# Second-layer row terms by way of VectorE and DRAM in place of TensorE, from batch 18 on

## The chip, the cores and the metric

The kernel runs on one core of a Trainium2 chip. The core has a matrix engine (TensorE, PE in the profile, with its weight loads as PEld), a vector engine (VectorE, DVE), an activation engine (ScalarE, ACT), a general-purpose engine (GpSimd, POOL) and SyncE (SP), which here issues most DMAs. Each engine runs its own instructions in order and waits on semaphores. DMAs from all queues share 16 DMA engines. The metric is the device time of one execution in microseconds; the comparison is between medians of several runs.

## The reference

The input `x` is 64 batches of 256 rows by 256 columns, with one 256x256 adjacency matrix for all. Two layers follow each other; in each, a graph attention and then a feed-forward part are added to `x`, each fed by a layer norm. What matters here is the attention of the second layer:

```
h = matmul(inp, W)                                  # 256 x 256 per batch
e_src = h @ a1;  e_dst = h @ a2                     # one number per row
e = leaky_relu(e_src[:, :, None] + e_dst[:, None, :], 0.01)
e = where(adj == 0, -1e9, e)
h_prime = matmul(softmax(e, -1), h);  out = relu(h_prime)
```

The feed-forward part of the first layer is a linear map, that of the second a mixture of eight experts of which each row uses its best two. All numbers are 32-bit floats.

## The kernel before

A batch is held as two row tiles of 128 rows (`NT` = 2) and two column tiles (`KT` = 2). The function `batch_layers` (L594) is a generator that does all of one batch's attention and linear work; its `yield` values are ranks. A main loop (L1241) advances in steps. Every third step a new batch starts, and in each step every active generator advances once, in the order of the ranks: a positive rank ends its part of the step, a negative one puts it back into the same step's queue at that rank. So the order of instructions on each engine is fixed when the program is built, several batches overlap, and the ranks alone set it. Three batches' stages stand in one round of three steps.

The row terms. Since exp is monotone, exp(leaky_relu(s + d)) is the larger of two products, exp(s)exp(d) and exp(0.01 s)exp(0.01 d). With a factor pulled out, each score is `max(term_of_column_row, number_of_partition) * mask`. The first operand of the max must be a row of 256 numbers that is the same in all 128 partitions, though `projected1` (L497) makes it as one number per partition (`ex[:, t, 1]`, L511). `scores1` (L520) turns it round: for each of the two tiles TensorE transposes the column, broadcast along the free axis to 128x128, against the identity into a PSUM bank `pd` (L523). VectorE then makes the scores of both tiles (L528), with `pd`, the partition's own number and the pre-scaled mask `me` (L517).

The first layer, with four heads, does the same thing by another way for all but the first batch. VectorE transposes the terms in 32x32 blocks into a small tile `ut` (L537, `send_terms`), a DMA stores them in DRAM (L621) and a second DMA reads the stored row into all 128 partitions at once with a stride of zero (L554, `rows_to_all`, 512 KB), into the last part of the score tile `z` that it is later overwritten in. Then VectorE makes the scores (L570). From batch 18 on (`SETTLED`, L129) both DMAs go through SP's queue, before that through ScalarE's.

Around the scores. VectorE's order in one round is, in the settled part: the scaling of the first layer's q (L485), the transpose L537, the statistics of a newer batch (L378, L379), the expert outputs y (L993), the expert inputs' transposes sT (L117), the second layer's scores (L528), the first layer's attention results (L591, L639), the second layer's residual (L694), the linear part's result x2 (L667), and so on to the first layer's scores (L570). ScalarE takes the exponential of L639's result (L645), the weighting of y (L961), the squares for the norm of x2 (L424) and the copy of the transposed x2 (L459). TensorE multiplies that copy in L504 (`projected1`), and then continues with the first layer's projection (L469), expert products (L968 hidden, L983 out), the transposes L523 and the attention sums (L584).

SP's order in one round: x in blocks (L106), the store of the terms (L621), the next x (L96), the read of the terms (L554), the store of a base (L734), then the loads of two expert pairs (L906 in four parts, L917, and their weights L935). A DMA of SP also waits for the DMA that stands eight before it.

Of the kernel before, what the change touches and what calls it, by code (L numbers as in the profile page):

```python
# [9 lines left out]
F32 = mybir.dt.float32  # L10
I32 = mybir.dt.int32
AF = mybir.ActivationFunctionType
ALU = mybir.AluOpType
AX = mybir.AxisListType

P = 128
# [5 lines left out]
def rows_to_all(ap: bass.AP, n: int) -> bass.AP:  # L22

    return bass.AP(tensor=ap.tensor, offset=ap.offset, ap=[[0, P], [1, n]])
# [3 lines left out]
def kernel(  # L28
# [17 lines left out]
    nc = tc.nc  # L46
    B, N, D = x.shape
# [4 lines left out]
    NT = N // P  # L52
# [21 lines left out]
    work = ctx.enter_context(tc.tile_pool(name="work", bufs=2))  # L74
    small = ctx.enter_context(tc.tile_pool(name="small", bufs=4))
# [3 lines left out]
    def bank(name, shape):  # L79
        t = psum.tile([P, 2 * D], F32, tag="bank", name=name, bufs=8)  # L80
        n = 1
        for s in shape:
            n *= s
        t = t[:, :n]
        if len(shape) == 2:
            t = t.rearrange("p (a b) -> p a b", a=shape[0])
        elif len(shape) == 3:
            t = t.rearrange("p (a b c) -> p a b c", a=shape[0], b=shape[1])
        return t
# [22 lines left out]
    S = 32  # L112
    G = P // S
# [15 lines left out]
    SETTLED = CHUNKS[0] + CHUNKS[1] + CHUNKS[2] + CHUNKS[3] + 2  # L129


    ident = const.tile([P, P], F32, tag="ident", name="ident")
# [186 lines left out]
    def once(work):  # L319
# [14 lines left out]
        out=tri, in_=tri, pattern=[[1, P]], base=0, channel_multiplier=-1,  # L334
# [157 lines left out]
    for i in range(2):  # L492
        t = keep.tile([P, NT, D + 1], F32, tag=f"q1_{i}", name=f"q1_{i}")
# [3 lines left out]
    def projected1(xT, rstd, b):  # L497

        q = q1s[b % 2]
        pqs = []  # L500
        for t in range(NT):
            pq = bank("pq", [D + 3])
            for k in range(KT):
                nc.tensor.matmul(  # L504
                    pq, xT[:, k, t * P : (t + 1) * P], wx1[:, k, :],
                    start=(k == 0), stop=(k == KT - 1),
                )
            pqs.append(pq)
        ex = small.tile([P, NT, 3], F32, tag="ex1", name="ex1")
        for t, pq in enumerate(pqs):  # L510
            nc.scalar.activation(ex[:, t, :], pq[:, D:], AF.Exp, scale=rstd[:, t : t + 1])  # L511
            nc.scalar.activation(
                q[:, t, :D], pq[:, :D], AF.Copy, scale=rstd[:, t : t + 1]
            )
        me = work.tile([P, NT, N], F32, tag="me", name="me", bufs=1)
        for j in range(NT):
            nc.scalar.activation(me[:, j, :], masks[1][:, j, :], AF.Copy, scale=ex[:, j, 0:1])  # L517
        return q, ex, me

    def scores1(ex, me):  # L520
        pd = bank("pd", [N])
        for t in range(NT):
            nc.tensor.transpose(  # L523
                pd[:, t * P : (t + 1) * P], ex[:, t, 1:2].to_broadcast([P, P]), ident
            )
        z = work.tile([P, NT, N], F32, tag="z1", name="z1", bufs=1)
        for j in range(NT):
            nc.vector.scalar_tensor_tensor(  # L528
                z[:, j, :], pd, ex[:, j, 2:3], me[:, j, :], op0=ALU.max, op1=ALU.mult
            )  # L530
        return [z[:, j, :] for j in range(NT)]

    def send_terms(q, b):


        ut = small.tile([P, S], F32, tag="ut", name="ut", bufs=1)
        nc.vector.transpose(  # L537
            ut.rearrange("p (t h w) -> p t h w", t=NT, h=H), q[:, :, :, HD - 1 : HD + 3]
        )
        ud = tc.dram_tile([S, S], F32, name=f"terms_{b}")  # L540
        ud = ud.rearrange("c r -> (c r)").rearrange("(c p) -> c p", p=P)
        return ut, ud
# [51 lines left out]
    def batch_layers(b, c0, xng, lg):  # L594
# [23 lines left out]
        if b:  # L618
            ut, ud = send_terms(q, b)
            yield -31  # L620
            terms_queue(b).dma_start(  # L621
                out=ud.rearrange("c (g r) -> g c r", g=G),
                in_=ut[2 : P : S // (NT * H), :],
            )
            yield -52
        z = work.tile([P, NT, NT, H, P], F32, tag="z4", name="z4", bufs=2)
# [17 lines left out]
        ex = work.tile([P, NT, D], F32, tag="e", name="e", bufs=1)  # L644
# [21 lines left out]
        for t in range(NT):  # L666
            nc.vector.scalar_tensor_tensor(  # L667
                x2[:, t, :], pf[:, t, :], rstd[:, t : t + 1], x1b[:, t, :],
                op0=ALU.mult, op1=ALU.add, accum_out=sums[:, t : t + 1],
# [6 lines left out]
        xT = transposed(x2)  # L676
        yield 20
        q, ex, me = projected1(xT, rstd, b)
        yield 25
        z = scores1(ex, me)  # L680
        yield 40
        pvs, rinv = attended(
            q[:, :, None, :], 1, lambda j, h, t: z[j][:, t * P : (t + 1) * P]
# [9 lines left out]
        for t in range(NT):  # L693
            nc.vector.scalar_tensor_tensor(  # L694
                x2[:, t, :], x2[:, t, :], 1.0, rel[:, t, :],
                op0=ALU.mult, op1=ALU.add, accum_out=sums[:, t : t + 1],
# [36 lines left out]
        if not dense:  # L733
            d = nc.sync.dma_start(  # L734
                out=out_rows[b * N : (b + 1) * N, :].rearrange("(t p) d -> p t d", p=P), in_=base
# [476 lines left out]
    def jobs():  # L1212
        b = done = taken = 0
        for c, nb in enumerate(CHUNKS + (1,) * DENSE):
            nt = nb * NT
            lg = keep.tile([P, nt, E], F32, tag="lg", name=f"lg_{c}", bufs=7)
            xng = []
            row0 = b * N
            done += nt
            n = max(done - (E - 1) - taken, 0) if b < ROUTED else 0  # L1220
            taken += n
            for i in range(nb):
                def job(b=b, c=c, i=i, nb=nb, nt=nt, n=n, lg=lg, xng=xng, row0=row0):
                    yield from batch_layers(b, i * NT, xng, lg)
                    if i == nb - 1:
                        if b >= ROUTED:
                            yield 65
                            yield from route_dense(b, lg)
                        else:
                            yield from route(c, row0, nt, n, b == ROUTED - 1, xng, lg)  # L1230
                yield job()
                b += 1
# [85 lines left out]
```

## Time and profile before

| | |
|---|---|
| median of 3 runs | 1486.76 us (1486.3 to 1491.11) |
| profiled execution | 1489.83 us |
| its span | 1488.0 us |
| granted TensorE clock | 0.985 of full |
| busy, share of span | PE 95%, PEld 85%, DVE 83%, ACT 68%, POOL 58% |
| L523, transposes `pd` | 128, mean 278 ns |
| L528, scores of the second layer | 128, mean 460 ns |
| L537, block transposes of the first layer | 63, mean 212 ns |
| L570, scores of the first layer, from z | 504, mean 482 ns |

Busy times are of one profiled execution. A record of a matmul is longer than its share of the engine, since matmuls overlap; what one costs in a dense stretch is the distance between starts. Instructions that only issue DMAs or wait are not counted as busy. In lists of waits the name behind the arrow is what came last.

### The profile page before, as it was taken

The numbers are of one execution on the slowest core, as the hardware profiler recorded it, in microseconds if no ns is written. First come the engines' busy times: TensorE is split into PE (matmuls) and PEld (weight loads), VectorE is DVE, ScalarE is ACT, GpSimd is POOL, SyncE is SP. The second block draws the span as 40 slices with busy tenths as digits, with TensorE's granted clock in tenths as the row PEclk, the third lists the DMA queues.
The fourth block names the chain that finished last, engine by engine and source line by source line (L and its number), as shares of the span: only waits on it lengthen the run. The fifth ranks groups of instructions, "written<-read, shape, count | busy, mean of one in ns | idle before, by whom it ended". The sixth has DMA issues, their size and how long they took to land. (4 is left out here: it accounts for less than half of the span.)

```text
span 1488.0 us, 29865 instructions
## 1 busy us (share of the span) xinstructions
PE 1420.1 (95%) x8138; PEld 1264.0 (85%) x8138; DVE 1232.9 (83%) x4320; ACT 1006.5 (68%) x2389; POOL 864.6 (58%) x851
## 2 busy tenths in 40 slices
PE   6899999999999999999999999999999999899994
PEld 5688888898999999899999989888888888778883
DVE  7689999988898889899888989998888888765442
ACT  1377667577777777777777787777777878643330
POOL 2122446455857676666758585776666668544444
PEclk9899999999999999999999999999999999999998
DMA  4832243567878777787877687768877786988743
GB/s 128 227 98 86 89 130 117 146 172 153 199 171 193 161 177 170 171 185 180 190 156 190 147 193 168 190 164 186 193 158 172 153 173 128 213 201 150 152 66 49
DMA packets 354081, 236.10 MB, mean 159 GB/s; under 512 B 246260, under 2 KB 316156, under 8 KB 353916
## 3 DMA queue, kind: packets, MB, share of 16 engines
q1 hardware_dynamic: 301000, 157.90, 42.1%
q0 software_dynamic: 48864, 66.33, 23.9%
q10 hardware_dynamic: 4052, 9.98, 2.3%
q8 instruction: 67, 1.10, 0.3%
q14 instruction: 98, 0.80, 0.2%
HBM read 146.00 MB, written 88.09 MB: 157 GB/s over the span
## 5 line engine op out<-in xcount | busy, mean ns | idle before, releaser
L1004 POOL DMA_INDIRECT out_dram<-y,xt x258 | 415.6, 1611 | 214.6 <-issue 54.6
L584 PE MATMUL pv<-q,z 128*128 128x65 f32 (+1 forms) x2560 | 363.7, 297 | 0.7 <-DVE z L570 0.3
L584 PEld LDWEIGHTS pv<-q,z 128*128 128x128 f32 x2560 | 331.2, 193 | 13.3 <-DVE z L570 1.3
L1066 POOL DMA_INDIRECT xs<-xng,pos x244 | 256.3, 1050 | 65.2 <-issue 57.7
L983 PE MATMUL py<-w2s,hT 128*128 (+1 forms) x1224 | 282.9, 382 | 4.7 <-ACT hT L974 4.5
L983 PEld LDWEIGHTS py<-w2s,hT 128*128 128x128 f32 x1224 | 229.7, 191 | 37.2 <-ACT hT L974 7.4
L570 DVE SCALAR_TENSOR_TENSOR z<-z,q,mask 128x256 f32<-128x256 f32 x504 | 231.5, 482 | 15.5 <-DMA z<-terms 6.5
L968 PE MATMUL ph<-sT,we 128*128 128x256 f32 x1032 | 241.4, 383 | 1.6 <-DVE sT L117 0.9
L968 PEld LDWEIGHTS ph<-sT,we 128*128 128x128 f32 x1032 | 195.6, 192 | 28.7 <-DVE sT L117 1.4
L961 ACT ACTIVATE y<-y,w 128x256 f32<-128x256 f32 x258 | 113.4, 499 | 119.4 <-DVE y L993 119.2
L459 ACT COPY xT<-pt 128x512 f32<-128x512 f32 x209 | 121.2, 588 | 82.1 <-PE pt L453 80.0
L974 ACT ACTIVATE hT<-ph,we 128x256 f32<-128x256 f32 x306 | 124.1, 472 | 64.1 <-PE ph L968 46.7
L406 POOL TENSOR_SCALAR rstd<-mv 128x4 f32<-128x4 f32 (+1 forms) x66 | 15.9, 240 | 224.8 <-DVE mv L379 175.3
L504 PE MATMUL pq<-wx,xT 128*128 128x259 f32 x512 | 126.5, 390 | 13.9 <-ACT xT L459 13.9
L424 ACT ACTIVATE off<-x,sums 128x256 f32<-128x256 f32 x256 | 129.2, 505 | 9.2 <-DVE x L667 3.3
L993 DVE TENSOR_TENSOR y<-py,b2s 128x512 f32<-128x512 f32 x129 | 86.9, 687 | 56.3 <-PE py L983 44.8
L469 PE MATMUL pq<-wx,xT 128*128 128x268 f32 x512 | 128.1, 394 | 2.4 <-DVE xT L117 1.2
L504 PEld LDWEIGHTS pq<-wx,xT 128*128 128x128 f32 x512 | 96.0, 192 | 33.6 <-ACT xT L459 19.8
L660 PE MATMUL pf<-wfT,xT 128*128 128x256 f32 x512 | 124.2, 386 | 0.0
L469 PEld LDWEIGHTS pq<-wx,xT 128*128 128x128 f32 x512 | 97.9, 192 | 21.7 <-DVE xT L117 1.4
L688 ACT ACTIVATE rel<-pv,rinv 128x256 f32<-128x256 f32 x128 | 54.0, 469 | 82.1 <-DVE rinv L591 81.8
L660 PEld LDWEIGHTS pf<-wfT,xT 128*128 128x128 f32 x512 | 94.9, 196 | 10.6
(170 smaller groups left out, 2355.7 us busy)
## 6 DMA issues: line engine op xcount, KB each, us to landing
we<-wpack SPq DMA_DIRECT2D x145, 288.0 KB
xr<-xs SPq DMA_DIRECT2D x516, 64.0 KB
z<-terms SPq DMA_DIRECT2D x46, 512.0 KB
xin<-in_x_dram SPq DMA_DIRECT2D x64, 256.0 KB
out_dram<-base SPq DMA_DIRECT2D x61, 256.0 KB
xblk<-in_x_dram SPq DMA_DIRECT2D x188, 64.0 KB
z<-terms ACTq DMA_DIRECT2D x17, 512.0 KB
out_dram<-y,xt POOLq DMA_INDIRECT x258
```

Source lines behind the costliest of these rows:

```text
L424: nc.scalar.activation(off, src[:, t, :], AF.Square, bias=sums[:, t : t + 1], scale=-float(D), accum_out=sq[:, at + t : at + t + 1],)
L459: nc.scalar.copy(dst, pt)
L469: nc.tensor.matmul(pq.rearrange("p h c -> p (h c)"), xT[:, k, t * P : (t + 1) * P], wx[:, k, :], start=(k == 0), stop=(k == KT - 1),)
L504: nc.tensor.matmul(pq, xT[:, k, t * P : (t + 1) * P], wx1[:, k, :], start=(k == 0), stop=(k == KT - 1),)
L570: nc.vector.scalar_tensor_tensor(z[:, j, :, h, :], terms, q[:, j, h, HD + 2 : HD + 3], masks[0][:, j, :].rearrange("p (t i) -> p t i", t=N ...
L584: nc.tensor.matmul(pv[:, h, :], z(j, h, t), q[:, j, h, : d + 1], start=(j == 0), stop=(j == NT - 1),)
L660: nc.tensor.matmul(pf[:, t, :], xT[:, k, t * P : (t + 1) * P], wfT[:, k, :], start=(k == 0), stop=(k == KT - 1),)
L968: nc.tensor.matmul(ph[:, f, :], we[:, k * D + f * P : k * D + (f + 1) * P], xT[:, k, :], start=(k == 0), stop=(k == KT - 1),)
L974: nc.scalar.activation(hT[:, f, :], ph[:, f, :], AF.Gelu, bias=we[:, C_B1 + f : C_B1 + f + 1])
L983: nc.tensor.matmul(py[:, t, :], hT[:, f, t * P : (t + 1) * P], w2s[:, e, f * D : (f + 1) * D].rearrange("p e c -> p (e c)"), start=(f == 0 ...
L1004: d = nc.gpsimd.indirect_dma_start(out=out_rows, out_offset=bass.IndirectOffsetOnAxis(ap=xt[:, t, 0:1].bitcast(I32), axis=0), in_=y[:, t, ...
L1066: d = nc.gpsimd.indirect_dma_start(out=xs_d[: E * CAP * PAIR, :], out_offset=bass.IndirectOffsetOnAxis(ap=at, axis=0), in_=xe, in_offset=None,
```

## The change

From batch 18 on the second layer's terms take the way of the first layer's. `scores1` gets the score tile `z` from outside and a flag `spread`, and where it is set it reads the terms from the last part of `z` instead of making `pd`. A new function `turned_terms1` transposes them in blocks on VectorE. Two DMAs on SP's queue are added: a store of 1 KB to a DRAM tile of its own for each batch, and a read of that row into all partitions (128 KB). The order in which VectorE, ScalarE, GpSimd and TensorE work on the rest is the same as before; the block transpose stands behind L537, and on SP the new store stands before the first layer's store, the new read before the first layer's read.

```diff
+    def turned_terms1(ex, b):
+        ut = small.tile([P, S], F32, tag="ut1", name="ut1", bufs=1)
+        nc.vector.transpose(
+            ut.rearrange("p (t w) -> p t w", t=NT),
+            ex[:, :, 1:2].to_broadcast([P, NT, S // NT]),
+        )
+        return ut, tc.dram_tile([N], F32, name=f"terms1_{b}")
...
-    def scores1(ex, me):
-        pd = bank("pd", [N])
-        for t in range(NT):
-            nc.tensor.transpose(
-                pd[:, t * P : (t + 1) * P], ex[:, t, 1:2].to_broadcast([P, P]), ident
-            )
-        z = work.tile([P, NT, N], F32, tag="z1", name="z1", bufs=1)
+    def scores1(ex, me, z, spread):
+        terms = z[:, NT - 1, :]
+        if not spread:
+            terms = bank("pd", [N])
+            for t in range(NT):
+                nc.tensor.transpose(
+                    terms[:, t * P : (t + 1) * P], ex[:, t, 1:2].to_broadcast([P, P]), ident
+                )
         for j in range(NT):
             nc.vector.scalar_tensor_tensor(
-                z[:, j, :], pd, ex[:, j, 2:3], me[:, j, :], op0=ALU.max, op1=ALU.mult
+                z[:, j, :], terms, ex[:, j, 2:3], me[:, j, :], op0=ALU.max, op1=ALU.mult
             )
...
         q, ex, me = projected1(xT, rstd, b)
-        yield 25
-        z = scores1(ex, me)
+        spread = b >= SETTLED
+        if spread:
+            yield -26
+            ut, ud = turned_terms1(ex, b)
+            yield -31
+            nc.sync.dma_start(
+                out=ud.rearrange("(t g r) -> g t r", t=NT, g=G),
+                in_=ut[0 : P : S // NT, :],
+            )
+            yield -52
+        z = work.tile([P, NT, N], F32, tag="z1", name="z1", bufs=1)
+        if spread:
+            nc.sync.dma_start(out=z[:, NT - 1, :], in_=rows_to_all(ud, N))
+        yield 45 if spread else 25
+        z = scores1(ex, me, z, spread)
```

## The prediction

> **What bounds the kernel now.** I read first the busy times by stretch (columns: stretch, busy us and instructions of PE, PEld, DVE, ACT, POOL, granted clock, DMA share, GB/s), then the timeline of one batch in each stretch.
>
> ```profile
> 330.00:931.00 601.00, 601.00 (x3575) 544.52 (x3574) 538.16 (x1840) 460.76 (x1087) 403.93 (x386) 1.00 0.77 175
> 931.00:1214.00 283.00, 274.23 (x1576) 243.13 (x1575) 249.73 (x901) 216.86 (x485) 195.12 (x181) 1.00 0.77 174
> 1214.00:1488.00 274.00, 240.22 (x1152) 207.34 (x1150) 159.14 (x578) 125.15 (x293) 143.05 (x109) 0.96 0.70 139
> ```
>
> Stretch A (batches 18 to 47) has no idle TensorE at all; TensorE is the bound and VectorE has 10% to spare. Stretch B (48 on) has idle TensorE. The rest is a tail, TensorE dense from 1320 to 1440 us, then scatters: time gained or lost in A and B passes through it whole.
>
> What one pair of removed transposes occupies is seen in the timeline of A (start, busy us, instruction):
>
> ```profile
> 707.52 3.62 PE L983 MATMUL py<-w2s,hT 128*128 x16
> 710.98 0.38 PE L523 MATMUL pd<-ident,ex 128*128 128x128 f32 x2
> 711.20 3.68 PE L584 MATMUL pv<-q,z 128*128 128x65 f32 x32
> ```
>
> Each record is 0.27 us long, but the next group starts 0.22 us after the first of the pair. The slot, not the record, is what removal gives back; it is 0.218 us in every batch of A.
>
> The same batch on the other side, where the new path will run:
>
> ```profile
> 709.24 0.21 DVE L537 STREAM_TRANSPOSE ut<-q 128x32 f32<-128x32 f32 x1
> 709.48 0.55 SPq L621 DMA_DIRECT2D terms<-ut  x1
> 710.07 0.45 SPq L96 DMA_DIRECT2D xin<-in_x_dram  x1
> 712.38 0.35 SPq L554 DMA_DIRECT2D z<-terms  x1
> 714.82 0.83 DVE L528 SCALAR_TENSOR_TENSOR z<-pd,ex,me 128x256 f32<-128x256 f32 x2
> ```
>
> Call T0 the end of L537 (709.45). VectorE wants the second layer's terms at T0+5.4 here. Over A this need cycles through 5.3, 5.3, 4.7 and 4.3 us.
>
> One batch of B, and the waits of 931 to 1214 us (waiter <- releaser: us, times, longest):
>
> ```profile
> 1117.27 0.21 DVE L537 STREAM_TRANSPOSE ut<-q 128x32 f32<-128x32 f32 x1
> 1121.01 0.83 DVE L528 SCALAR_TENSOR_TENSOR z<-pd,ex,me 128x256 f32<-128x256 f32 x2
> 1125.03 0.69 DVE L993 TENSOR_TENSOR y<-py,b2s 128x512 f32<-128x512 f32 x1 [0.42 <-PE py L983]
> 1130.89 0.56 ACT L459 COPY xT<-pt 128x512 f32<-128x512 f32 x1
> 1131.74 1.91 PE L504 MATMUL pq<-wx,xT 128*128 128x259 f32 x8
> ...
> PEld pq L504 <- ACT xT L459: 12.0, 10, 2.6
> PE pq L504 <- ACT xT L459: 8.1, 5, 2.2
> ```
>
> The need is only T0+3.5 to 4.4 here, and L528 leads through L639 or L993 and ScalarE's queue (L645 or L961, then L424, L459) to TensorE's L504. In most of batches 48 to 59 L504 starts 0.05 us after its copy ends: no slack.
>
> **What the skill says.** "Perfetto Trace Analysis", Identifying the Most-Contended Engine, holds that matmul busy time misleads, because matmuls are pipelined; agreed, 0.27 against 0.11 us per transpose. "DMA: Bandwidth & Descriptors", Anatomy of one DMA, prices a transfer at 2.0 us and its bytes at 436 GB/s (fitted on GpSimd's path). The semaphores' updates in this trace show 1.66 to 2.9 us from issue to landing for `terms<-ut`, 3.0 for the 256 KB `xin` and 5.0 for the 512 KB `z<-terms` (medians), so the page's 3.2 us for the last is too little under load. The same page, Two DMAs through the same engine are not ordered: a read of what a DMA wrote must wait for its completion; L554 does (2.9 us after L621 above), and the new read will.
>
> **The change, part by part.** *Removed:* 46 pairs at 0.218 us of TensorE, 10.0 us at most. The freed bank only loosens later waits for banks; A has none.
>
> *VectorE:* one transpose per batch behind L548. L537, of the same 128x32 size, is 0.21 us, and its successor starts 0.13 later: 0.13 us each. The two score operations now read SBUF: 0.48 (L570 from z) against 0.46 to 0.47 from PSUM, 0.04 us a batch. From 610 to 690 us, four batches, VectorE's timeline is idle 8.5 us, 2.1 a batch; 1.3 of these are waits for TensorE or ScalarE that can be used up, the rest gaps between dependent small operations; so 0.17 us, and 0.22 of a shorter period, are covered.
>
> *SP:* the order of the new program per batch is: new write, old write, `xin`, new read, old read. With 0.55, 0.55 and 0.45 us and gaps of 0.05, the new read can go at T0+1.95, or, if later, when its write has landed: T0+0.27+W, W the batch's `terms` landing of 1.66 to 2.9. All behind it (the 512 KB read, the store of base, the xr, xt and we loads) goes about 1 us later. SP waits some 7 us a batch for VectorE, z lands 4 to 6.5 us before L570, and xr and we are used a batch later: no cost. With cover gone for the 512 KB read, a late z would stop L570 microsecond for microsecond.
>
> *The read:* 128 KB in 1 KB rows. The page's formula gives an estimate of 2.3 us, `xin`'s 256 KB row 3.0; it queues behind `xin`, so I take 2.9, and 2.4 from batch 58, where `xin` is gone. It lands at T0+4.85 where W is small, up to 5.9 where large.
>
> *Stalls in A:* need plus 0.13 is 5.4, 5.4, 4.8, 4.4; W is 2.8, 2.8, 1.7, 1.7. Landings with W=2.8 are near 5.6 (packets already flow behind `xin`), else 4.85: stalls of 0.1 to 0.2, 0.1 and 0.4. Slack from L528 to L504 is 0.5, 1.15, 0.95, 0.95 us, less the 0.22+0.17 of this change. Only the first kind (8 batches) is at its limit; I charge 0.5 us in all. A: -30 x 0.218 + 0.5 = -6.0.
>
> *Stalls in B.* Needs after T0 of batches 48 to 60: 4.3, 6.1, 4.4, 4.3, 3.9, 3.4, 3.5, 3.4, 3.5, 3.4, 4.2, 3.4, 4.2; W: 1.7, 2.1, 1.7, 2.2, 2.0, 1.7, 1.9, 1.7, 2.7, 2.0, 2.9, 2.5, 1.9. Landing less need (plus 0.13), less idle VectorE or slack behind it: batch 48 0.4; 49 none (need 6.2); 50 0.3; 51 0.95-0.5; 52 hidden by a ScalarE backlog of 1.2; 53 1.3-0.2; 54 and 55 hidden (waits for pv, pf and py of 2.2 and 2.0); 56 2.25-0.7; 57 1.6-0.2; 58 1.3; 59 1.6-0.2; 60 and 61 hidden; 62 none; 63 some 0.3, hidden. Sum 7.9, and 8 batches x 0.13 for the transpose = 1.0. What goes late next: L504 and all TensorE work behind it. Gain in B: pd lies before L504, which waits for ScalarE, so the slot is worth nothing except in batches 54, 55, 60, 61, 62: -1.1. B: +7.8.
>
> Sum +1.8 us on the profiled run's 1489.8 us (span 1488.0): +0.12%. Median of runs 1486.8, so 1488.5 us.
>
> Unknowns, both ends. The read: 2.3 (page) to 3.4 us. Landing 0.5 us later costs 0.5 in nine batches of B (4.5) and in A, past its slack, 0.45 in each of the two tight kinds, 15 batches (7): +11.5. Landing 0.5 earlier gives back 4 in B and 0.5 in A: -4.5. The added traffic, 6 MB on 236 MB: 0 to 2 us. The write's 0.55 us of issue may be less with 8 rows in place of 32: 0 to -0.3 a batch, inside those ends. A bank freed: 0 to -1.
>
> **Rivals.**
> *Faster:* the stalls stay off the path: 1486.8-7.6 = 1479.2 with A's slots and the five of B, 1476.8 if all 46 count. For it: VectorE is idle 10%, and it waits for TensorE in places after L528. Against it: L504's 0.05 us. It decides if the read lands within 1.6 us of its issue in B; the smallest landing of any load here, 64 KB, is 1.9.
>
> *Slower:* one mechanism, the read lands 0.5 us later than I take it, for it shares the rings with `xin` and the scatters. From T0+5.0 in batches with small W A's slack is used up and VectorE's lateness reaches TensorE there too: 1488.5+11.5 = 1500. For it: `z<-terms` takes 5.0 where the page says 3.2. Against it: the rings carry little between the terms and the base store.
>
> *The big read is late instead:* L570 waits. It has 4 to 6 us in hand and loses 1: 1488.5 unchanged. That the change doesn't do what it says is excluded: the program has 46 transposes, writes and reads more, 92 matmuls fewer, all else in the same order.
>
> **How the numbers follow.** Two runs of this kernel differ by some 0.3% (4.5 us: 1482.3 to 1491.2 counts as no change). The likeliest case, 1483 to 1493 and chance 0.5, lies with a tenth of it above that bound; the slower rival 0.32, around 1500; the faster 0.18, around 1478.5. So faster 0.18, same 0.45, slower 0.37. The range must reach into both rivals: 1479 to 1502 leaves out half of the faster one's and a third of the slower one's chance, 0.2.
>
> **What would show it.** The span of A (batch 18's to 48's L537) shorter by 6 us; that of B longer by 8; waits of VectorE's second-layer score operation for DMA z<-terms of 0.1 to 0.5 us in A and 1 to 2 us in B, about 25 us in all; L504's waits for its copy up by some 8 us; the new read issued at T0+2 to 3 and landing 2.4 to 3.0 us later; L570 without new waits. I am wrong if the read lands earlier than VectorE asks (faster), or if TensorE shows idle time in A (slower).

## The result and the profile after

The changed kernel takes 1548.68 us (median of 6 runs, 1539.83 to 1552.46), the kernel before on the same chip 1488.88 (6 runs, 1486.3 to 1493.08). The ratio is 1.0396, with a 95% interval of 1.0363 to 1.0429: slower by about 60 us, where 1488.5 was predicted with a range up to 1502. The profiled execution took 1547.86 us, its span is 1546.1.

In the changed kernel the lines are shifted: L523 is the new block transpose on VectorE, L695 the new store, L702 the new read, L539 the second layer's scores (L528 before). L537, L554, L570, L584, L621, L639 and L645 are now L548, L565, L581, L595, L632, L650 and L656. Lines up to L513 keep their numbers.

To place the difference I mark the start of each batch's first transposes `xng` on TensorE, which come once per batch, and call the stretch between the 17th and the 47th of these marks A, from there to the 59th B1, to the 64th B2. A is the prediction's A, B1 and B2 its B. (In us; the tail ends with TensorE's last matmul.)

| | up to A | A | B1 | B2 | tail | after TensorE's end | span |
|---|---|---|---|---|---|---|---|
| before | 334.4 | 600.6 | 282.7 | 96.4 | 155.2 | 18.7 | 1488.0 |
| after | 331.8 | 636.4 | 306.0 | 99.8 | 159.3 | 12.8 | 1546.1 |
| difference | -2.6 | +35.8 | +23.3 | +3.4 | +4.1 | -5.9 | +58.1 |

A should have become 6 us shorter and became 36 us longer. The busy times by stretch of the changed kernel answer to the prediction's first view (same columns):

```profile
332.00:968.00 636.00, 604.38 (x3511) 539.96 (x3511) 545.07 (x1869) 461.15 (x1086) 409.32 (x383) 0.99 0.76 171
968.00:1274.00 306.00, 283.43 (x1550) 248.76 (x1549) 251.22 (x916) 218.88 (x486) 199.75 (x184) 0.96 0.74 167
1274.00:1546.00 272.00, 240.55 (x1116) 205.31 (x1114) 156.59 (x568) 121.87 (x287) 139.36 (x105) 0.95 0.70 141
```

TensorE, which had no idle time in A, now has 31.6 us of it. The work of the other engines has hardly changed (VectorE 545 us where it had 538 plus 30 new transposes). The granted clock, the third number from the end, fell to 0.96 in the second stretch, where it had been 1.00.

The timeline of the same batch as in the prediction, in all engines:

```profile
709.82 0.17 DVE L523 STREAM_TRANSPOSE ut<-ex 128x32 f32<-128x32 f32 x1
710.01 0.59 SPq L695 DMA_DIRECT2D terms<-ut  x1
710.93 3.68 PE L595 MATMUL pv<-q,z 128*128 128x65 f32 x32
711.78 0.39 SPq L702 DMA_DIRECT2D z<-terms  x1
716.83 1.01 DVE L539 SCALAR_TENSOR_TENSOR z<-z,ex,me 128x256 f32<-128x256 f32 x2 [2.46 <-DMA z<-terms]
717.97 0.75 DVE L650 TENSOR_TENSOR hp<-pv,rinv 128x256 f32<-128x256 f32 x2
718.76 0.63 ACT L656 ACTIVATE e<-hp 128x512 f32<-128x512 f32 x1 [3.02 <-DVE hp L650]
723.10 1.57 ACT L998 ACTIVATE hT<-ph,we 128x256 f32<-128x256 f32 x4
724.54 0.60 ACT L459 COPY xT<-pt 128x512 f32<-128x512 f32 x1
725.20 1.14 PE L504 MATMUL pq<-wx,xT 128*128 128x259 f32 x4 [1.87 <-ACT xT L459]
```

L595 follows without the transposes ahead of it, so the slot is gone. The read is issued at 711.78, 1.89 us after T0, as the prediction had it (1.95). But VectorE, which comes to the scores 2.46 us too early, stands until 716.8: the read needed some 5 us. From there the lateness goes on as the prediction's path said: L650, ScalarE's exponential (L656), its queue up to the copy L459, and L504, which leaves TensorE idle for 1.87 us. Before the change the same exponential (then L645) waited 0.55 us and L504 not at all:

```profile
716.57 0.63 ACT L645 ACTIVATE e<-hp 128x512 f32<-128x512 f32 x1 [0.55 <-DVE hp L639]
723.43 1.92 PE L504 MATMUL pq<-wx,xT 128*128 128x259 f32 x8
```

The waits of the whole run after (us in total, times, longest):

```profile
ACT e L656 <- DVE hp L650: 89.8, 46, 4.6
DVE z L539 <- DMA z<-terms: 68.9, 42, 3.3
PEld pq L504 <- ACT xT L459: 62.3, 45, 4.1
PE pq L504 <- ACT xT L459: 47.2, 37, 3.7
DVE z L581 <- DMA z<-terms: 4.5, 2, 2.3
```

and those of before for three of them:

```profile
ACT e L645 <- DVE hp L639: 22.6, 31, 3.1
PE pq L504 <- ACT xT L459: 13.9, 9, 2.8
DVE z L570 <- DMA z<-terms: 6.5, 2, 4.2
```

VectorE's new wait is 68.9 us, ScalarE's for VectorE grew by 67, TensorE's for the copy by 33. L581 (L570 before), behind the big read, has no new wait.

The updates of semaphores in the trace give the landing of each DMA. The new read lands 4.40 us after its issue (median over 46 batches; a tenth under 3.6, a tenth over 4.7), where the prediction took 2.9. From here on T0 is counted, in the changed kernel and its variants, from the end of the new transpose L523, which is 0.1 us later than the prediction's T0. So counted, the read is issued at T0+1.74 and lands at T0+6.26 (medians). In the prediction's own count that is T0+1.83 and T0+6.38, and it had 1.95 and 4.85.

### The profile page after: what moved, and what is told of

Same layout as the page of the kernel before. It is cut to its first block, busy times and chain, and to the rows that moved or that the text cites. A ratio compares the mean times of both kernels' runs of the same rounds, so it can differ in the third digit from the quotient of the medians.

```text
span 1546.1 us, 29839 instructions
## 1 busy us (share of the span) xinstructions
PE 1435.4 (93%) x8046; PEld 1266.7 (82%) x8046; DVE 1242.6 (80%) x4366; ACT 1008.0 (65%) x2389; POOL 874.5 (57%) x851
## 5 line engine op out<-in xcount | busy, mean ns | idle before, releaser
L595 PE MATMUL pv<-q,z 128*128 128x65 f32 (+1 forms) x2560 | 366.2, 298 | 0.3
L595 PEld LDWEIGHTS pv<-q,z 128*128 128x128 f32 x2560 | 335.8, 194 | 15.2 <-DVE z L581 0.9
L992 PE MATMUL ph<-sT,we 128*128 128x256 f32 x1032 | 244.8, 387 | 3.8 <-DVE y L1017 2.5
L581 DVE SCALAR_TENSOR_TENSOR z<-z,q,mask 128x256 f32<-128x256 f32 x504 | 231.4, 481 | 13.5 <-DMA z<-terms 4.5
L504 PE MATMUL pq<-wx,xT 128*128 128x259 f32 x512 | 136.4, 412 | 47.4 <-ACT xT L459 47.2
L459 ACT COPY xT<-pt 128x512 f32<-128x512 f32 x209 | 121.3, 588 | 71.3 <-PE pt L453 69.2
L504 PEld LDWEIGHTS pq<-wx,xT 128*128 128x128 f32 x512 | 98.8, 201 | 76.5 <-ACT xT L459 62.3
L469 PEld LDWEIGHTS pq<-wx,xT 128*128 128x128 f32 x512 | 100.4, 197 | 22.7 <-DVE wx L168 1.3
L656 ACT ACTIVATE e<-hp 128x512 f32<-128x512 f32 x64 | 40.4, 631 | 111.1 <-DVE hp L650 89.8
L453 PE MATMUL pt<-ident,x 128*128 128x128 f32 x512 | 84.6, 281 | 24.9 <-DVE x L678 24.9
```

What stands on the lines that cost most here:

```text
L459: nc.scalar.copy(dst, pt)
L469: nc.tensor.matmul(pq.rearrange("p h c -> p (h c)"), xT[:, k, t * P : (t + 1) * P], wx[:, k, :], start=(k == 0), stop=(k == KT - 1),)
L504: nc.tensor.matmul(pq, xT[:, k, t * P : (t + 1) * P], wx1[:, k, :], start=(k == 0), stop=(k == KT - 1),)
L581: nc.vector.scalar_tensor_tensor(z[:, j, :, h, :], terms, q[:, j, h, HD + 2 : HD + 3], masks[0][:, j, :].rearrange("p (t i) -> p t i", t=N ...
L595: nc.tensor.matmul(pv[:, h, :], z(j, h, t), q[:, j, h, : d + 1], start=(j == 0), stop=(j == NT - 1),)
L992: nc.tensor.matmul(ph[:, f, :], we[:, k * D + f * P : k * D + (f + 1) * P], xT[:, k, :], start=(k == 0), stop=(k == KT - 1),)
```

## The experiments

**Theories.** *The read is late*: the read of one row into 128 partitions takes some 4.4 us by itself, VectorE's lateness comes from that, and all else is as predicted. *Traffic*: the new DMAs slow the others, or delay SP, and TensorE's stalls are a sum of these. *Slots are worth less* than 0.218 us, so that there was nothing to gain. All edits are to the changed kernel unless said otherwise, and ratios are against the kernel before on the same chip. A ratio and its interval are estimated from all of the runs compared; the two medians beside it can differ from it by some 0.2%.

**e1, no terms at all** (an edit to the kernel before).

```diff
-        pd = bank("pd", [N])
-        for t in range(NT): nc.tensor.transpose(pd[...], ...)
+        pd = masks[1][:, 0, :]        # from batch 18 on
```

> From batch 18 on the second layer's scores take a constant row in SBUF in place of the row terms: no transposes on TensorE, none on VectorE, no DMA, no wait. The output leaves the row terms out. It prices what the removal of the 46 pairs is worth alone. By the slot of 0.218 us: 7.6 us (A's 30 batches and five of B) to 10.0 us (all 46), so 1479 to 1481 us against 1488.9. If removal is worth more than the slot, by the 0.27 us records of two transposes each, it is 25 us: 1464.

Measured: 1477.86 us (4 runs) against 1487.28, ratio 0.9911 (0.9882 to 0.9939). A is 594.0 us, 6.6 shorter, B1 unchanged, B2 1.3 shorter. This is what the slots are worth in this profile: 30 x 0.218 us in A, little in B. The ratio allows 9 to 18 us, somewhat more than these stretches add up to (7.9); what is left is not placed. The third theory falls.

**e2, the new path beside the old one.** All of the new path runs, but the scores come from `pd` as before, and are written into `me`, so nothing waits for the read.

```diff
-        terms = z[:, NT - 1, :]
-        if not spread:
-            terms = bank("pd", [N])
+        terms = bank("pd", [N])       # in all batches; scores go into me where spread
...
-        yield 45 if spread else 25
+        yield 25
```

> The kernel before, with the new path beside it and unused: VectorE's transpose, the store and the 128 KB read run from batch 18 on, into a tile that nobody reads; TensorE's transposes give the terms, and the scores are written in place into me. Theory 1 (the wait of VectorE for the read is the loss): about the time before, 1487 to 1494. Rival (the added DMAs slow the rest, or SP's issues make others late): most of the 60 us stays, over 1520.

Measured: 1490.51 us (12 runs) against 1487.28, ratio 1.0015 (0.9999 to 1.0030). The read still lands 4.26 us after its issue, and nobody waits. A is 600.6, the same as before; B1 is 2.4 longer, but 6.8 us of it ran at half of TensorE's clock, and none before (more on this clock below), so the added work need not be the reason. So transposes, stores, reads and SP's longer queue cost 0 to 4.5 us in all. The theory of traffic falls as the main cause: the loss is the wait.

**e3, 128 rows in place of one.** The read takes 128 different rows of `x`, with the same size, place, packets of 1 KB and wait for the store.

```diff
-            nc.sync.dma_start(out=z[:, NT - 1, :], in_=rows_to_all(ud, N))
+            d = nc.sync.dma_start(out=z[:, NT - 1, :], in_=x_rows[b * N : b * N + P, :])
+            tc.add_manual_dep(d.ins, stored.ins.name, AFTER, ...)
```

> The changed kernel, but the 128 KB read takes 128 different rows of x, each to its own partition, with the same wait for the store before it. The output has wrong terms. Theory 1a (the read is slow because 128 packets ask for the same 1 KB of DRAM): it lands 2.5 to 3.0 us after its issue in place of 4.4, VectorE's waits fall from 69 us to under 15, time 1485 to 1500. Rival 1b (it is slow because it stands behind x's 256 KB and beside the 512 KB read in the rings): landing still 4.0 or more, time 1540 to 1552.

Measured: 1495.98 us (5 runs), ratio 1.0043 (1.0019 to 1.0067). The read lands 2.67 us after its issue, at T0+4.80. The waits:

```profile
DVE z L539 <- DMA z<-in_x_dram: 15.4, 18, 1.7
PE pq L504 <- ACT xT L459: 19.7, 16, 4.3
```

15.4 us in place of 68.9. A is 597.9, 2.7 below before, B1 is 293.1, 10.4 above. This is close to the kernel that the prediction had computed: landing 4.85, A -6.0, B +7.8, in sum +1.8; measured some 6 to 9 us of loss. So most of the miss lies in one number, the duration of this read, and that depends on what it reads. Its place in the queue and its neighbours are those of the changed kernel, so they are not what makes that one slow.

**e4, 16 copies of the row in DRAM.** Two stores put 16 copies of the terms into DRAM, and each copy is read by 8 partitions.

```diff
... (the store, now two DMAs with 16 copies each of half a row)
-                in_=rows_to_all(ud, N)
+                in_=bass.AP(tensor=ud.tensor, offset=ud.offset, ap=[[N, COPIES], [0, P // COPIES], [1, N]])
```

> The changed kernel, but the store writes 16 copies of the 1 KB row (in two DMAs of 64 runs of 128 bytes), and each group of 8 partitions reads its own copy. Theory 1a: landing of the read near 3 us, but the second store costs SP 0.6 us more ahead of it, so VectorE's waits fall to 20 to 35 us; time 1495 to 1520. Rival 1b: landing 4.4 and 0.6 later than now, time 1555 to 1575.

Measured: 1527.21 us (4 runs), ratio 1.0268 (1.0237 to 1.0299). The read lands in 2.78 us, but it is issued at T0+2.56, 0.8 later than with one store, so it lands at T0+5.5, and VectorE waits for it 46.7 us in all. The mechanism holds, the expected time doesn't: what the copies save is partly spent ahead of the read.

**e5, the scores a step later.**

```diff
-        yield 45 if spread else 25
+        yield 99 if spread else 25
+        if spread:
+            yield 5
         z = scores1(ex, me, z, spread)
-        yield 40
+        yield -40 if spread else 40
```

> The changed kernel, but the second layer's scores come a step later: on VectorE behind x2 (L678) and the block transpose xT, ahead of the sum x (L659), and TensorE's use of them stays where it was. The read may then land some 9 us after T0 without a wait; nothing is taken away. If the wait is the whole loss: VectorE's waits for the read fall from 69 us to under 5, and the time comes to that of the run without terms, 1478, plus what VectorE's transposes cost, so 1478 to 1485. If the slow read also hurts in other ways (later loads, rings), 1490 or more.

Measured: 1486.37 us (22 runs) against 1486.70 (35), ratio 0.9998 (0.9986 to 1.0011). The read still takes 4.23 us, and VectorE doesn't wait for it. A is 6.1 shorter; B1 and B2 are 3.4 and 2.0 longer, and TensorE's attention sums now wait 8.4 us for the scores:

```profile
PE pv L595 <- DVE z L539: 8.4, 11, 1.5
```

So the loss is gone, but the time stays just above the expected 1478 to 1485: what A gains is given back behind it.

**e6, one row that is old.** Is it that the row has just been written? The read takes one row of `x`, the input, into all partitions.

```diff
+    ROWS = 1
-            nc.sync.dma_start(out=z[:, NT - 1, :], in_=rows_to_all(ud, N))
+            row = x_rows[b * N : b * N + ROWS, :]
+            ... in_=bass.AP(tensor=row.tensor, offset=row.offset, ap=[[N, ROWS], [0, P // ROWS], [1, N]])
```

> The changed kernel, but the read takes one row of x, stored long before, for all 128 partitions, with the same wait for the store. The output has wrong terms. Theory 1a (one 1 KB asked for by 128 packets): landing 4.0 to 4.6 us, time 1540 to 1552, as with the terms. Rival 1c (it is slow because the row was written just before): landing near 2.7 as with 128 rows of x, time near 1496.

Measured: 1569.26 us (4 runs), ratio 1.0530 (1.0488 to 1.0571), landing 4.74 us.

```profile
L540 DVE SCALAR_TENSOR_TENSOR z<-z,ex,me 128x256 f32<-128x256 f32 x92 | 44.7, 486 | 88.9 <-DMA z<-in_x_dram 86.8
```

(costliest groups: busy us, mean ns | idle before, most of it released by). The landing and the time are even above what was expected: an old row is as slow as a new one, or slower. It is not the freshness. What e6 shares with the changed kernel, and e3 doesn't, is that all 128 reads are of one row.

**e7, four rows**, each read by 32 neighbouring partitions (`ROWS = 4` in the edit of e6).

> As the run with one row of x, but four rows, each read by 32 partitions. Theory 1a: between the one row's 4.4 and the 128 rows' 2.7 us, about 3.2; time between 1496 and 1548, about 1510. Rival 1c: as with 128 rows, 1496.

Measured: 1551.82 us (4 runs), ratio 1.0427 (1.0390 to 1.0464), landing 4.26 us where I had expected 3.2. A miss, with a second cause in it. The semaphore of this read takes an early step at 1.0 us after the issue and then four landings from 3.6 us on; that of the changed kernel has no early step and 16 landings. The Trainium skill, "DMA: Bandwidth & Descriptors", in Why a DMA increments its semaphore by 16 and not by 1, says that a DMA uses the largest number of engines up to 16 that divides the slowest dimension (of a size other than 1) of both of its access patterns, and that the rest of the 16 is written at once. The trace agrees: the pattern began with a 4, and there are four landings, so four engines did it all. The run doesn't tell what four rows cost with 16 engines.

**e8, only the rank.** The scores go behind the results of the linear part, in the same step.

```diff
-        yield 45 if spread else 25
+        yield 72 if spread else 25
```

> The changed kernel with rank 72 in place of 45 for the scores: the same step, behind x2 on VectorE, about 3 us later than now. If the wait is the whole loss, the landing at T0+6.3 is just in time in stretch A (asked for at T0+8) and nearly so in B: waits under 8 us in all, 1478 to 1487. If the place of the scores matters by itself, since TensorE's attention sums wait for them, more than 1490.

Measured: 1488.77 us (14 runs) against 1486.70, ratio 1.0004 (0.9987 to 1.0021). The read lands in 4.12 us. By stretch:

```profile
331.00:926.00 595.00, 595.00 (x3520) 539.24 (x3519) 542.23 (x1870) 460.57 (x1086) 401.22 (x384) 1.00 0.79 183
926.00:1212.00 286.00, 273.22 (x1551) 242.15 (x1551) 251.94 (x919) 219.08 (x489) 195.94 (x184) 0.99 0.78 179
```

and by waits:

```profile
PE pq L504 <- ACT xT L459: 15.9, 12, 3.3
DVE z L539 <- DMA z<-terms: 0.2, 1, 0.2
```

TensorE is full in A again, and A is 6.3 us shorter than before, with the slow read in place. Moving one stage by 2 to 3 us of VectorE's work takes away all that the change lost, against the changed kernel some 60 us. In B1 and B2 3.0 and 2.5 us are given back, so that the time, 1488.77, lies between the two expectations. Of these e2, where nothing waits, shows 2.4 and 0.5 as well, so the added work itself may cost this there. Or it is the clock: in B1 e2 has 6.8 us at half clock, e8 3.4, the kernel before none. Single profiles don't settle it.

**e9, in A alone.** As e8, and the new path ends where TensorE is no longer full.

```diff
-        spread = b >= SETTLED
+        spread = SETTLED <= b < 46
```

> The scores at rank 72, so that no wait is left, and the new path for batches 18 to 45 alone; from 46 on TensorE transposes the terms as in the kernel before. If stretch A gives 0.218 us a batch and the loss of stretch B is what the new path costs there: A shorter by 6.1 us, B as before, 1480 to 1482 against 1486.7, ratio 0.996. If the gain in A is given back in B whatever B does, 1485 to 1488.

Measured: 1499.58 us (8 runs) against 1505.29 (13 runs of the kernel before on this chip, which is slower than the others here), ratio 0.9938 (0.9912 to 0.9964). It beats the kernel before by 6 us by the medians and 9 by the ratio, 5 to 13 by its interval. The slots of its 28 batches promise 6.1. That the gain lies in A is not shown: no profile of the kernel before was taken on this chip, and this run's A, 603.0 us, can't be compared with the 600.6 of a faster one.

**e10, e11 and e12, which rows are shared by whom.** These read rows of `x`: e10 16 rows, each into 8 neighbouring partitions (the pattern of e6 with `ROWS = 16`); e11 and e12 have the two dimensions exchanged, so that partition p reads row p mod 16, or p mod 8.

```diff
-                    ap=[[N, ROWS], [0, P // ROWS], [1, N]],
+                    ap=[[0, P // ROWS], [N, ROWS], [1, N]],     # ROWS = 16 in e11, 8 in e12
```

> As the run with one row of x, but 16 rows, each read by 8 neighbouring partitions, as the 16 copies of the terms were. If what counts is how many partitions ask for one 1 KB: landing near 2.8 us, as with the copies; four rows gave 4.3. If the copies were quick for another reason, 4 or more.

> The same 16 rows of x, but partition p reads row p mod 16, so that neighbours ask for different rows, and each row is again read 8 times. If the number of different rows counts: landing near 2.8 us as with neighbours on one row. If what slows the read is that several DMA engines ask for one row at the same moment: 3.5 to 4.5.

> As the read of the 16 rows shared, but with 8 rows of x (partition p reads row p mod 8), so that the access pattern's slowest dimension is 16 and not 8: the semaphore of the read should rise by 16 landings, not by one early step and 8. Each row is read 16 times, once for each eighth of a group of neighbouring partitions. The numbers in the scores are wrong ones, everything else is as in the changed kernel. If a read is slow because all 16 shares of it ask for the same row at the same moment, each share goes through the same 8 rows in the same order and the read lands 4.2 to 4.8 us after its issue, the time is 1.035 to 1.05 of the kernel before. If only the number of reads of one row counts (16 here, 8 in the run with 16 rows of 8 neighbours, 128 in the changed kernel), it lands near 3.0 us and the time is 1.005 to 1.015. If the slow landing of the 16 rows shared (3.9) came from its 8 shares alone, it is near 3.0 as well.

Measured, one run each, so that their ratios have no interval: e10 1522.04 and e11 1552.99 us against 1505.29 on their chip, e12 1517.66 against 1488.58 (one run too) on its own. All reads together (landings are medians; waits are those of VectorE's second-layer scores for the read, in sum):

| | reads of one row | DMA engines | issue to landing | T0 to landing | waits | ratio |
|---|---|---|---|---|---|---|
| e3, 128 rows | 1 | 16 | 2.67 | 4.80 | 15.4 | 1.004 |
| e10, 16 rows | 8 | 16 | 2.90 | 5.06 | 27.7 | 1.011 |
| e12, 8 rows shared | 16 | 16 | 3.32 | 5.36 | 37.0 | 1.020 |
| e4, 16 copies | 8 | 16 | 2.78 | 5.50 | 46.7 | 1.027 |
| e11, 16 rows shared | 8 | 8 | 3.89 | 5.76 | 46.4 | 1.032 |
| e7, 4 rows | 32 | 4 | 4.26 | 6.16 | 69.6 | 1.043 |
| after, 1 row | 128 | 16 | 4.40 | 6.26 | 68.9 | 1.040 |
| e6, 1 old row | 128 | 16 | 4.74 | 6.58 | 86.8 | 1.053 |

e10 lands as expected if the number of partitions on one row counts. e11 has the early step too and used 8 engines, so it leaves its question open; e12 puts it with 16 engines, and lands between the two expectations, at 3.3. With 16 engines the landing grows with the number of reads of one row: 2.7 for one, 2.8 to 2.9 for 8, 3.3 for 16, 4.4 to 4.7 for 128. With 128 reads in all, more reads of one row also means fewer different rows, and these runs can't tell the two apart. Whether it counts that the engines ask for one row at the same moment stays open too. What the table settles is the kernel: whatever sets the landing, the ratio follows the landing after T0, from 4.8 to 6.6 us, with one exchange of neighbours (e7 and the changed kernel).

How lateness becomes time can be read by stretch. In A the idle time of VectorE just before these scores sums to 6.1 us in e3, 22.4 in e4, 44.7 after and 50.1 in e6. A's length plus the 6.5 us of removed slots, less before, is 3.8, 19.8, 42.3 and 52.8. Nearly every microsecond of VectorE's wait is one of TensorE's.

## Why the prediction was wrong

**The bound and the slots** were right: e1's A is 6.6 us shorter (6.5 predicted), its B 1.3 (1.1 predicted). One reading goes the other way: the Trainium skill, in the section that the prediction cites ("Perfetto Trace Analysis", Identifying the Most-Contended Engine), says that pipelined matmuls look smaller in the trace, and here a transpose's record (0.27 us) is longer than its slot (0.11). Busy time misleads, but by showing too much.

**VectorE's added work** in A (0.17 us a batch, covered) was right: e2's A is unchanged, e8's keeps 6.3 of the 6.5.

**SP's order** was right: the read is issued 1.83 us after the prediction's T0, 1.95 was predicted. DMAs behind it land a little later (the 512 KB read 5.8 us after its issue, 5.0 before; the store of base likewise 5.8 and 5.0), and L581 doesn't wait for that.

**The read is the step that failed**: "it queues behind `xin`, so I take 2.9, and 2.4 from batch 58, where `xin` is gone". It lands 4.40 us after its issue. The queue isn't the reason: e3's read stands at the same place in it and lands in 2.67, and batches 62 and 63 of the changed kernel, with neither `xin` nor the big read near, still take 3.6 and 4.1. It was priced by size, from a row that reads 256 different rows and from a formula for bytes. The formula of the Trainium skill ("DMA: Bandwidth & Descriptors", Anatomy of one DMA) gives 2.3 us as an estimate, and the read of 128 different rows does take 2.67. But the new read has another form, one row into all partitions, and two rows of that form stood in the trace of before: `b2s`, also 128 KB, landed in 3.0 us at the least and 4.0 at the median of its eight loads, and the 512 KB `z<-terms` in 5.0 where the formula gives 3.2. The prediction quoted the latter, even as an argument for its slower rival, and took its upper bound at 3.4 all the same.

**Stalls in A**, 0.5 us charged, measured about 42. Put the landing of A, 6.39 us after the prediction's T0 (median), into its own working: it exceeds the needs of 5.4, 5.4, 4.8 and 4.4 by 0.99, 0.99, 1.59 and 1.99 us, and the slack of 0.5, 1.15, 0.95 and 0.95 less 0.39 leaves 0.88, 0.23, 1.03 and 1.43 us, on average 0.89, or 27 us in 30 batches. So the landing explains nearly two thirds of A. The rest is slack that wasn't there: in A nearly all of the waits pass through. e3 shows this term by itself: its landing is close to the predicted one, and A still lost 3.8 us where 0.5 was charged. The working let each batch start with its slack whole, while VectorE, with 545 us of work and 45 of idle time before these scores in 636, has too little room left to catch up between two waits. This reason is argued from the sums, no run isolates it.

**Stalls in B**: +7.8 us predicted for B, measured +23.3 in B1 and +3.4 in B2. Here a second term was missing altogether: the clock. One place in B, TensorE's timeline, after:

```profile
1097.95 1.89 PE L1007 MATMUL py<-w2s,hT 128*128 x8
1103.56 3.82 PE L504 MATMUL pq<-wx,xT 128*128 128x259 f32 x8 [3.72 <-ACT xT L459]
```

and the stretches around it (columns as above, granted clock third from the end):

```profile
1091.00:1102.50 11.50, 8.84 (x47) 7.56 (x46) 10.76 (x39) 6.71 (x14) 7.21 (x6) 1.00 0.97 250
1102.50:1109.30 6.80, 5.74 (x13) 4.54 (x14) 6.26 (x26) 5.41 (x14) 5.84 (x6) 0.50 0.76 156
1109.30:1121.00 11.70, 11.70 (x74) 10.69 (x73) 7.86 (x30) 7.73 (x18) 8.53 (x9) 1.00 0.74 163
```

L504's eight matmuls take 3.82 us, twice the 1.91 of one in the prediction's view. After a gap of 3.7 us TensorE is granted half of its clock for 6.8 us. In A and B1 this happens nowhere before the change; after it, 6.8 us of A and 23.9 of B1 are at half, and TensorE is busy in 6.5 and 22.5 of them. That is at most 3.3 and 11.3 us of lost work. B1 then nearly adds up: 13.8 us more idle time than before, 11.3 for the clock, less 2.6 for 12 removed slots, is 22.5 of 23.3. A doesn't quite: 31.6 + 3.3 - 6.5 is 28.4 of 35.8, and the other 7 us are in matmuls that the profile counts as busy; what slows these stays open.

**The rivals.** The slower one named the right path and the right point ("From T0+5.0 in batches with small W A's slack is used up and VectorE's lateness reaches TensorE there too"): e3 at T0+4.80 still gains in A, e12 at 5.36, on a chip where the kernel before takes the same time, loses 11.5 there. Its reason, rings shared with `xin` and the scatters, is not what e3 and e6 show, and its size, half a microsecond, was a third of the real 1.5. The faster one's gain in A comes when the read is not asked for so early (6.3 us in e8), but only e9 keeps it in the whole time. The big read's lateness cost nothing, as said.

**What would show it.** A wait of VectorE for `z<-terms` of about 25 us in all was said, it is 69; L504's waits up by 8, it is 33; "I am wrong ... if TensorE shows idle time in A (slower)" is the sign that came, with 31.6 us.

## What to carry to other kernels

Price a DMA by a row of the trace that has its form (how many partitions read the same bytes, how many engines share it), and let the range reach to that row, before any formula for its size. Where a removed operation is replaced by a round trip through DRAM, first move the consumer behind other work of its engine: here one rank was worth some 60 us. Even then the whole time was no better than before (e8), and a gain was left only with the change kept to the stretch where the engine it relieves has no idle time (e9). When a stall is new on a full TensorE, count its clock too, not the gap alone.

## What the runs showed of the hardware

- One 1 KB row read into 128 partitions by 16 DMA engines lands after 4.4 to 4.7 us, 128 different rows after 2.7. In the batch shown, 35 packets of 1 KB are on record between T0+3.75 and T0+5.5. Half of them took over 200 ns and the longest 644, where such packets take 46 ns otherwise (median), and seven 4 KB packets of the big read that began meanwhile took 1.0 to 2.1 us in place of 0.16. Over all batches, from 2 us after the issue to the landing, one 1 KB packet in ten took over 195 ns; in e3 nine in ten took 46.
- A source pattern whose slowest dimension is 4 or 8 was moved by 4 (e7) or 8 (e11) DMA engines, seen as an early step of its semaphore at 1.0 to 1.1 us and then 4 or up to 8 landings.
- TensorE's clock halves for 3.41 us or a multiple of it (6.83 in the place shown, 10.24 in e6). The Trainium skill, "TensorE: Matmul & The Clock Gate", Part 1: The HAM clock gate, says that this comes after an idle window of about 3.4 us. Here less is enough: of the seven drops between 332 and 1274 us after the change, the longest gap of the 9 us before each was 1.9 to 3.7 us, and five of them were under 2.6. Nor does such a gap always do it: after two others in that time, of 1.9 and 2.1 us, the clock stayed full.
